# Window attention in a four-layer network: score tiles of 32 rows by 64 columns, value tiles of 32 columns, head parity in place of window as the unit

## The chip, the cores and the metric

The kernel runs on one core of a Trainium2 chip. A core has five engines that work side by side, each through its own list of instructions in order: TensorE (PE; PEld is its weight load), VectorE (DVE), ScalarE (ACT), GpSimd (POOL) and SyncE (SP), which here only loads registers and issues DMA transfers. They meet through semaphores. The metric is the device time of one execution in microseconds, the median of several runs; lower is better.

## What is computed

Four images of 256 channels by 64 by 64 points pass through four layers, each added to its input after a group normalisation: two attention layers and two state-space (Mamba) layers. The change is in the attention layers alone. What matters of their reference:

```python
xw = to_windows(x_img)                    # 8 by 8 windows of 64 points
qkv = xw @ qkv_w.T + qkv_b
q, k, v = (qkv[..., :C], qkv[..., C:2 * C], qkv[..., 2 * C:])
logit = einsum('bpc,bqc->bpq', q.mean(axis=2) * SCALE, k.mean(axis=2))
tk_logit, idx = top_k(logit, 4)           # each window reads 4 windows
k_g, v_g = ...                            # keys and values of these 4
# 8 heads of 32 channels, 64 queries, 4 * 64 keys
attn = softmax(einsum('bphqd,bphkd->bphqk', qh * SCALE, kh), axis=-1)
out = einsum('bphqk,bphkd->bphqd', attn, vh)
out_img = from_windows(out) + lepe(v)     # a 3x3 depthwise convolution of v
out_img = out_img @ wo_w.T + wo_b
```

So a window has 8 heads, and each head a score matrix of 64 queries by 256 keys with a contraction over 32 channels. Everything is float32.

## The kernel before

The images go one after the other (`net_kernel`). Each attention layer has a scan phase (`scan_phase`: recurrence, q, k and v by strips of 8 image columns; keys and values go to a DRAM buffer by window) and then a window phase (`window_phase`), which is where the change lies. There are 4 x 2 = 8 window phases in an execution.

The window phase takes 64 windows as 32 pairs; `i` is the pair, `w` (0 or 1) the window in it, `sj, a = divmod(i, 4)` the strip and the place in it. Channels lie on the 128 partitions in two halves `m`; within a half, `b` is the lower or upper 64 partitions, that is two heads. Per pair the steps are these.

- `indices` (L448) reads the four window numbers of each window into SP's registers; `gather` (L461) issues eight DMAs, four per window, into the tile `kv`, of which there are six. Keys of the four gathered windows lie so that window `j` is on partitions 64*(j mod 2) onward (`r = j % 2`).
- `scores` (L480) makes, for each window, a PSUM tile `sc[w]` of two banks: eight matmuls of 64 rows by 128 columns. The stationary operand is q of two heads side by side (`p h t`), 64 columns each. For this q is held in `qbuf` with a zero in the place of the other head (L105 writes the zeros once per image): a contraction over 64 rows with two heads in it then gives one head's scores in each 64 columns. Two of these matmuls (`r` = 0, 1) sit in different halves of the array's rows and write to different banks.
- `smallest` (L491) takes the minimum over the keys (q is stored negated), `exps` (L502) the exponential in four parts with its sum, into the tile `pr`, of which there are two; `normalise` multiplies by the reciprocal (L512 on DVE, L514 on POOL).
- `turn` (L528) transposes the weights in eight 128 by 128 blocks into two PSUM tiles `pt`; `turned` copies one on DVE (L539) and one on ACT (L541).
- `values` (L552) multiplies by the gathered values, 128 rows by 64 columns, 128 columns of weights moving: two heads' value columns against two heads' weights, so that half of what it makes (a head's values under the other head's weights) isn't used. `own_rows` (L565) therefore picks the used half in four DVE instructions of 32 partitions each and adds it to the image tile `vimg`. There is one PSUM tile `ov`.
- In 26 of the 32 pairs a matmul over a strip follows (`conv`, L208): either `project` of a finished strip, whose result DVE adds to x (L577, `add`), or `queries` for a coming strip, whose result four ACT instructions of 32 partitions write into q (L266, `evict`); SP then copies each half of q to the other partitions (L275, `double`). There are 12 pairs of the latter kind.

The work of a pair overlaps the next: in iteration `i` the loop issues the scores, minima, exponentials and normalisation of pair i + 1 and the turn, values and addition of pair i. The order on each engine is that of the loop, written by hand (L620 to L660): gather(i+2), double, indices(i+3), scores(i+1), smallest(i+1, 0), turn(i, 0), smallest(i+1, 1), exps(i+1, 0) first half, turned(i, 0), exps(i+1, 0) second half, own_rows(i-1), conv, normalise(i+1, 0), turn(i, 1), exps(i+1, 1) first half, turned(i, 1), exps(i+1, 1) second half, add, normalise(i+1, 1), evict, values(i, 0), values(i, 1), and then one or two of the 36 taps of the depthwise convolution that POOL does (L229, L230, L242). Steps of a group normalisation (`gn`, or `stats` in the second layer) are put between them in some pairs (`mids`, `ends`).

PSUM has eight banks: four for `sc`, two for `pt`, one for `ov`, one for `conv` and the normalisation.

Of the kernel before, what the change touches and what calls it, by code (L numbers as in the profile page):

```python
# [18 lines left out]
P = 128  # L19
NB = 4  # L20
C = 256
# [3 lines left out]
NH = 4  # L25
# [20 lines left out]
class Net:  # L46
# [33 lines left out]
    def attention_layers(self, x, w_drams, v_drams):  # L80
        tc, nc = self.tc, self.nc
        with ExitStack() as ctx:
# [17 lines left out]
                [big.tile([P, 2, NW, 2, 64], F32, name=f"q{i}{m}") for m in range(2)]  # L100
                for i in range(2)
            ]
            for t in qbuf[0] + qbuf[1]:
                for r in range(0, P, 32):
                    nc.gpsimd.memset(t[r : r + 32, :, :, 1 - r // 32 % 2, :], 0.0)  # L105
# [151 lines left out]
            def queries(lay, s, m, psum):  # L257
# [4 lines left out]
                def evict():  # L262
                    for h in range(NH):
                        rows = slice(h * 32, h * 32 + 32)
                        b, h2 = divmod(h, 2)
                        nc.scalar.activation(  # L266
                            q[rows, b, :, h2, :].rearrange("p w (j i) -> p w j i", i=8),
                            ps[rows].rearrange("p (j w i) -> p w j i", j=8, i=8),
                            AF.Identity, bias=lay["neg_bq"][rows, m : m + 1], scale=-SCALE,
                        )  # L270
# [163 lines left out]
            def window_phase(lay, work, psum, idx, nxt):  # L434
# [31 lines left out]
                sc = {}  # L466
# [3 lines left out]
                def scores(i):  # L470
                    sj, a = divmod(i, 4)
                    for w in range(2 if i < n_pair else 0):
                        sc[w] = psum.tile([P, 2, 4, P], F32, tag="sc", name="sc", bufs=2)
                        t = kv[i, w]
                        for cq in range(4):
                            m, b = divmod(cq, 2)
                            for r in range(2):
                                rows = slice(r * 64, r * 64 + 64)
                                k0 = b * P + m * 64
                                nc.tensor.matmul(  # L480
                                    sc[w][:, r, cq, :],
                                    qbuf[sj % 2][m][rows, b, 2 * a + w].rearrange("p h t -> p (h t)"),
                                    t[rows, :, k0 : k0 + 64], start=True, stop=True,
                                )

                mn = {}

                def smallest(i, w):
                    if i < n_pair:
                        mn[w] = self.small.tile([P, 4], F32, tag="mn", name="mn", bufs=4)  # L490
                        nc.vector.tensor_reduce(  # L491
                            mn[w], sc[w].rearrange("p r c n -> p c r n"), AX.XY, ALU.min
                        )

                def exps(i, w, part=range(4)):
                    if i < n_pair:
                        if 0 in part:
                            sm[i, w] = self.small.tile([P, 4], F32, tag="sm", name="sm", bufs=4)
                            pr[i, w] = work.tile([P, 4, 2, 2, 64], F32, tag="pr", name="pr", bufs=2)
                        t = pr[i, w]  # L500
                        for cq in part:
                            nc.scalar.activation(  # L502
                                t[:, cq].rearrange("p j r t -> p r j t"),
                                sc[w][:, :, cq, :].rearrange("p r (j t) -> p r j t", j=2),
                                AF.Exp, bias=mn[w][:, cq : cq + 1], scale=-1.0,
                                accum_out=sm[i, w][:, cq : cq + 1],
                            )

                def normalise(i, w):
                    if i < n_pair:  # L510
                        t, s = pr[i, w], sm.pop((i, w))
                        nc.vector.reciprocal(s, s)  # L512
                        t = t.rearrange("p c j r t -> p c (j r t)")
# [7 lines left out]
                def turn(i, w):  # L521
                    pt[w] = [
                        psum.tile([P, 4, P], F32, tag="pt", name="pt_ps", bufs=2) for j in range(2)
                    ]
                    t = pr.pop((i, w))
                    for j in range(2):
                        for cq in range(4):
# [1502 lines left out]
```

## Time and profile before

| | |
|---|---|
| median of 3 runs | 12441.65 us (12438.44 to 12444.25) |
| the profiled execution, its own time | 12439.35 us |
| span of its instructions | 12437.6 us, so 1.75 us lie around it |
| busy share of the span | PE 82%, DVE 82%, POOL 73%, ACT 58% |
| granted TensorE clock, mean | 0.922 |
| first to last scores of a window phase | 228.0 to 496.1 us in the first, 709.7 to 989.8 in the second |
| the same in the other six | 269.7, 281.5, 269.5, 278.3, 269.3 and 278.1 us long |

The eight window phases together are thus some 2200 of 12437.6 us; most of the rest belongs to the two state-space layers. In the page's slices a window phase is where ACT and POOL rise together (slices 2 and 3 of each quarter). The page names groups by line, so L480, L491, L502, L512, L514, L528, L539, L541, L552 and L565 are the attention loop. A line's mean is the time of one instruction as the profiler records it; matmuls overlap, so for PE the distance between starts is what counts, not the mean.

### The profile page before, as it was taken

Reading aid. Unit: us, or ns where it says so; the run is one execution under the profiler, and the core shown is the slowest. Engines: PE = TensorE matmul, PEld = TensorE weight load, DVE = VectorE, ACT = ScalarE, POOL = GpSimd, SP = SyncE. Lnnn points to the kernel's source line nnn. Section 1 sums busy time; section 2 is a strip of 40 time slices with the busy share of each in tenths; the row PEclk is TensorE's granted clock in tenths of the full one; section 3 lists DMA queues with packets and bytes.
Section 4 is the critical chain, followed back from the end, with each engine's and each line's share of the span. In section 5 each row is a group of like instructions: output and inputs, shape, how many; then the busy total and the mean of one; then the engine's idle time right before and its main releaser. Section 6 shows DMA issues by size and latency. Waiting matters only on the chain. (4 is left out here: it accounts for less than half of the span.)

```text
span 12437.6 us, 159552 instructions
## 1 busy us (share of the span) xinstructions
PE 10255.9 (82%) x54592; PEld 6015.9 (48%) x54592; DVE 10216.3 (82%) x9130; ACT 7245.9 (58%) x13300; POOL 9018.9 (73%) x4634
## 2 busy tenths in 40 slices
PE   8987887787898788777789878877878987887777
PEld 4664544443466454444346645444434664544443
DVE  6777898897677799889767779988976777998897
ACT  4565554776466555477645655547754565554775
POOL 4666886887466688688746668868874666886887
PEclk9999998999899999899889999989988999998998
DMA  3343554454334455454433434545543343554454
GB/s 96 108 128 131 168 169 147 167 169 142 97 108 127 132 169 170 146 168 167 144 95 109 127 130 172 169 146 167 169 142 95 109 127 130 172 170 146 167 170 140
DMA packets 680299, 1773.54 MB, mean 143 GB/s; under 512 B 89120, under 2 KB 195120, under 8 KB 678464
## 3 DMA queue, kind: packets, MB, share of 16 engines
q1 hardware_dynamic: 679488, 1763.34, 43.7%
q8 instruction: 435, 7.13, 0.2%
q14 instruction: 376, 3.08, 0.1%
HBM read 1601.51 MB, written 94.37 MB: 136 GB/s over the span
## 5 line engine op out<-in xcount | busy, mean ns | idle before, releaser
L926 POOL TENSOR_TENSOR hc<-h,cb 128x1024 f32<-128x1024 f32 x2056 | 4814.1, 2350 | 988.2 <-DVE h L920 425.6
L920 DVE TENSOR_TENSOR_SCAN h<-da,m_state,pb 128x1024 f32<-128x1024 f32 x1248 | 2919.9, 2340 | 161.7 <-DVE pb L914 2.8
L872 PE MATMUL y<-ident,hc 128*128 128x128 f32 x16384 | 2371.0, 293 | 346.7 <-POOL hc L926 259.0
L872 PEld LDWEIGHTS y<-ident,hc 128*128 128x128 f32 x16384 | 2091.8, 152 | 1009.7 <-POOL hc L926 439.0
L914 DVE TENSOR_TENSOR pb<-du,pb 128x1024 f32<-128x1024 f32 x1672 | 2024.8, 1211 | 92.5 <-PE pb L844 89.3
L856 ACT ACTIVATE da<-delta,m_v 128x1024 f32<-128x1024 f32 x1672 | 1898.8, 1141 | 220.8 <-DVE h L920 204.0
L844 PE MATMUL pb<-m_parts,pick 128*128 128x512 bf16 x3312 | 1099.8, 417 | 872.2 <-DVE h L920 821.8
L502 ACT ACTIVATE pr<-sc,mn 128x256 f32<-128x256 f32 x2048 | 956.6, 478 | 770.8 <-PE pt_ps L528 551.2
L514 POOL TENSOR_TENSOR pr<-pr,sm 128x1024 f32<-128x1024 f32 x512 | 967.9, 1897 | 560.0 <-DVE sm L512 380.6
L844 PEld LDWEIGHTS <-pick 128*128 128x128 bf16 x3312 | 255.2, 101 | 1883.1 <-DVE h L920 1160.3
L920 DVE TENSOR_TENSOR_SCAN h<-da,pb 128x1024 f32<-128x1024 f32 x424 | 969.6, 2287 | 55.6 <-DVE pb L914 1.4
L830 POOL TENSOR_TENSOR bb<-du,bb 128x1024 f32<-128x1024 f32 x376 | 888.8, 2364 | 65.2 <-DMA bb<-m_cd 60.5
L491 DVE TENSOR_REDUCE mn<-sc 128x4 f32<-128x1024 f32 x512 | 609.6, 1219 | 244.9 <-PE sc L480 242.8
L920 DVE TENSOR_TENSOR_SCAN h<-dap,m_state,bb 128x1024 f32<-128x1024 f32 x288 | 672.0, 2333 | 76.2 <-ACT dap L856 63.4
L528 PE MATMUL pt_ps<-ident,pr 128*128 128x128 f32 x4096 | 571.6, 283 | 145.7 <-ACT pts L541 64.3
L208 PE MATMUL conv_ps<-att_y,att_wb 128*128 128x512 f32 x1536 | 688.8, 593 | 0.0
L856 ACT ACTIVATE dap<-delta,m_v 128x1024 f32<-128x1024 f32 x376 | 419.6, 1116 | 422.3 <-DVE h L920 298.2
L552 PE MATMUL ov_ps<-pts,kv 128*64 128x128 f32 x8192 | 583.6, 289 | 91.6 <-DVE vimg L565 75.6
L480 PE MATMUL sc<-kv,q 64*128 64x128 f32 x8192 | 573.0, 288 | 81.7 <-DMA kv<-kv_dram 68.0
L528 PEld LDWEIGHTS pt_ps<-ident,pr 128*128 128x128 f32 x4096 | 465.8, 144 | 315.4 <-issue 151.4
L480 PEld LDWEIGHTS sc<-kv,q 64*128 64x128 f32 x8192 | 515.8, 196 | 124.3 <-issue 56.1
L552 PEld LDWEIGHTS ov_ps<-pts,kv 128*64 128x64 f32 x8192 | 456.4, 141 | 217.2 <-DVE vimg L565 131.9
(270 smaller groups left out, 18063.0 us busy)
## 6 DMA issues: line engine op xcount, KB each, us to landing
cb<-m_cd SPq DMA_DIRECT2D x2048, 512.0 KB
kv<-kv_dram SPq DMA_DIRECT2D x2048, 128.0 KB
bb<-m_cd SPq DMA_DIRECT2D x376, 512.0 KB
q<-q SPq DMA_DIRECT2D x256, 256.0 KB
kv_dram<-kst SPq DMA_DIRECT2D x128, 256.0 KB
kv_dram<-vn SPq DMA_DIRECT2D x128, 256.0 KB
x<-in_x_dram SPq DMA_DIRECT2D x8, 2048.0 KB
m_pe<-in_pe_dram SPq DMA_DIRECT2D x32, 512.0 KB
```

The source lines that it names most:

```text
L480: nc.tensor.matmul(sc[w][:, r, cq, :], qbuf[sj % 2][m][rows, b, 2 * a + w].rearrange("p h t -> p (h t)"), t[rows, :, k0 : k0 + 64], start= ...
L502: nc.scalar.activation(t[:, cq].rearrange("p j r t -> p r j t"), sc[w][:, :, cq, :].rearrange("p r (j t) -> p r j t", j=2), AF.Exp, bias=m ...
L514: nc.gpsimd.tensor_tensor(t, t, s.rearrange("p (a o) -> p a o", o=1).to_broadcast([P, 4, 256]), ALU.mult,)
L528: nc.tensor.transpose(pt[w][j][:, cq, :], t[:, cq, j].rearrange("p r t -> p (r t)"), self.ident,)
L552: nc.tensor.matmul(ov[i][b * 64 : b * 64 + 64, m, :, :, w, :], t[:, j, c0 : c0 + 64], pts[w][j][:, cq, :], start=(j == 0), stop=(j == 1),)
L830: nc.gpsimd.tensor_tensor(pb[i], slots[i][0]["du"], pb[i], ALU.mult)
L844: nc.tensor.matmul(pb[i][:, ss], self.pick[:, n : n + 1].to_broadcast([P, P]), blk["parts"][:, ss], start=True, stop=True,)
L856: nc.scalar.activation(da[i], blk["delta"], AF.Exp, scale=blk["a"](n))
L872: nc.tensor.matmul(blk["y"][:, ss], t[:, ss], self.ident, is_transpose=True, start=(n == 0 and ss.start % NT == 0), stop=(n == DS - 1 and ...
L914: nc.vector.tensor_tensor(pb[i], blk["du"], pb[i], ALU.mult)
L920: nc.vector.tensor_tensor_scan(h[i][:, ss], da[i][:, ss], pb[i][:, ss], state, ALU.mult, ALU.add)
L926: nc.gpsimd.tensor_tensor(hc[i][:, ss], h[i][:, ss], cb[i][:, ss], ALU.mult)
```

## The change

- q is held without zeros: `qbuf` has 64 columns per window instead of 128, the 16 memsets of L105 go, `evict` is two ACT instructions of 64 partitions instead of four of 32, and `double` moves half the bytes.
- The unit of `sc`, `mn`, `pr`, `sm`, `pt` and `pts` is no longer the window `w` but the head's parity `h`: each of the two now holds both windows of the pair. Its four parts are (w, m) instead of (m, b), and the two halves of its partitions are `b` instead of the two heads.
- `scores` makes 32 matmuls of 32 rows by 64 columns instead of 16 of 64 by 128; four row places (r, h) go to four different banks, two column places (b) to the two halves of the partitions. The two `sc` tiles are filled interleaved, all within one block.
- `values` is called once for a pair: 32 matmuls of 128 rows by 32 columns, 64 moving columns, instead of 16 of 128 by 64 with 128. All four heads of a half lie on their own 32 partitions of `ov`, which is half as large.
- `own_rows` is one DVE instruction of 128 partitions instead of four of 32.
- `pr` has four buffers instead of two.
- Sizes of the minima, exponentials, normalisation, transposes and copies stay as they are.

```diff
-                [big.tile([P, 2, NW, 2, 64], F32, name=f"q{i}{m}") for m in range(2)]
+                [big.tile([P, 2, NW, 64], F32, name=f"q{i}{m}") for m in range(2)]
                 for i in range(2)
             ]
-            for t in qbuf[0] + qbuf[1]:
-                for r in range(0, P, 32):
-                    nc.gpsimd.memset(t[r : r + 32, :, :, 1 - r // 32 % 2, :], 0.0)
...
-                    for h in range(NH):
-                        rows = slice(h * 32, h * 32 + 32)
-                        b, h2 = divmod(h, 2)
+                    for b in range(2):
+                        rows = slice(b * 64, b * 64 + 64)
                         nc.scalar.activation(
-                            q[rows, b, :, h2, :].rearrange("p w (j i) -> p w j i", i=8),
+                            q[rows, b].rearrange("p w (j i) -> p w j i", i=8),
...
                 def scores(i):
                     sj, a = divmod(i, 4)
-                    for w in range(2 if i < n_pair else 0):
-                        sc[w] = psum.tile([P, 2, 4, P], F32, tag="sc", name="sc", bufs=2)
-                        t = kv[i, w]
-                        for cq in range(4):
-                            m, b = divmod(cq, 2)
-                            for r in range(2):
-                                rows = slice(r * 64, r * 64 + 64)
-                                k0 = b * P + m * 64
-                                nc.tensor.matmul(
-                                    sc[w][:, r, cq, :],
-                                    qbuf[sj % 2][m][rows, b, 2 * a + w].rearrange("p h t -> p (h t)"),
-                                    t[rows, :, k0 : k0 + 64], start=True, stop=True,
-                                )
+                    if i < n_pair:
+                        for h in range(2):
+                            sc[h] = psum.tile([P, 2, 2, 2, P], F32, tag="sc", name="sc", bufs=2)
+                        for w in range(2):
+                            for m in range(2):
+                                for r in range(2):
+                                    for h in range(2):
+                                        r0 = r * 64 + h * 32
+                                        rows = slice(r0, r0 + 32)
+                                        for b in range(2):
+                                            k0 = b * P + m * 64
+                                            nc.tensor.matmul(
+                                                sc[h][b * 64 : b * 64 + 64, r, w, m, :],
+                                                qbuf[sj % 2][m][rows, b, 2 * a + w],
+                                                kv[i, w][rows, :, k0 : k0 + 64],
+                                                start=True, stop=True,
+                                            )
...
-                            pr[i, w] = work.tile([P, 4, 2, 2, 64], F32, tag="pr", name="pr", bufs=2)
+                            pr[i, h] = work.tile([P, 4, 2, 2, 64], F32, tag="pr", name="pr", bufs=4)
...
-                def values(i, w):
-                    if w == 0:
-                        ov[i] = psum.tile([P, 2, 2, 8, 2, 8], F32, tag="ov", name="ov_ps", bufs=1)
-                    t = kv.pop((i, w))
-                    for m in range(2):
-                        for j in range(2):
-                            for b in range(2):
-                                cq = 2 * m + b
-                                c0 = C + cq * 64
-                                nc.tensor.matmul(
-                                    ov[i][b * 64 : b * 64 + 64, m, :, :, w, :],
-                                    t[:, j, c0 : c0 + 64], pts[w][j][:, cq, :],
-                                    start=(j == 0), stop=(j == 1),
-                                )
+                def values(i):
+                    ov[i] = psum.tile([P, 2, 8, 2, 8], F32, tag="ov", name="ov_ps", bufs=1)
+                    for w in range(2):
+                        t = kv.pop((i, w))
+                        for m in range(2):
+                            for j in range(2):
+                                for h in range(2):
+                                    for b in range(2):
+                                        p0 = b * 64 + h * 32
+                                        c0 = C + m * P + p0
+                                        nc.tensor.matmul(
+                                            ov[i][p0 : p0 + 32, m, :, w, :],
+                                            t[:, j, c0 : c0 + 32],
+                                            pts[h][j][:, 2 * w + m, b * 64 : b * 64 + 64],
+                                            start=(j == 0), stop=(j == 1),
+                                        )
...
-                        for r in range(4):
-                            rows = slice(r * 32, r * 32 + 32)
-                            out = vimg[rows, :, 8 * sj : 8 * sj + 8, 1 + a * 16 : 17 + a * 16]
-                            nc.vector.tensor_tensor(
-                                out, ov[i][rows, :, r % 2].rearrange("p m j w i -> p m j (w i)"),
-                                out, ALU.add,
-                            )
-                        del ov[i]
+                        out = vimg[:, :, 8 * sj : 8 * sj + 8, 1 + a * 16 : 17 + a * 16]
+                        nc.vector.tensor_tensor(
+                            out, ov.pop(i).rearrange("p m j w i -> p m j (w i)"), out, ALU.add
+                        )
...
-                    values(i, 0)
-                    values(i, 1)
+                    values(i)
```

## The prediction

> **What bounds the kernel now.** The chain of waits that ends last covers only 17% of the span and lies in the last image's state-space layers, so it says nothing on the attention loop. I read the page's groups first for sizes, then the timeline of a few pairs for the order, then the waits, then the clock by windows. The page gives the loop's pieces:
>
> ```profile
> L502 ACT ACTIVATE pr<-sc,mn 128x256 f32<-128x256 f32 x2048 | 956.6, 478 | 770.8 <-PE pt_ps L528 551.2
> L514 POOL TENSOR_TENSOR pr<-pr,sm 128x1024 f32<-128x1024 f32 x512 | 967.9, 1897 | 560.0 <-DVE sm L512 380.6
> L552 PE MATMUL ov_ps<-pts,kv 128*64 128x128 f32 x8192 | 583.6, 289 | 91.6 <-DVE vimg L565 75.6
> L480 PE MATMUL sc<-kv,q 64*128 64x128 f32 x8192 | 573.0, 288 | 81.7 <-DMA kv<-kv_dram 68.0
> ```
>
> 8192 records are 32 for each of 256 pairs, where the code has 16 matmuls: each float32 matmul is two passes. ACT's largest wait is for the transposes: with two `pr` buffers an exponential can't be written before `turn` has read the one of a pair earlier. One pair in the timeline (start, length, engine, line):
>
> ```profile
> 407.85 2.06 PE L480 MATMUL sc<-kv,q 64*128 64x128 f32 x32
> 409.05 2.35 DVE L491 TENSOR_REDUCE mn<-sc 128x4 f32<-128x1024 f32 x2 [0.88 <-PE sc L480]
> 409.83 1.09 PE L528 MATMUL pt_ps<-ident,pr 128*128 128x128 f32 x8
> 410.76 1.88 PE L208 MATMUL conv_ps<-att_y,att_wb 128*128 128x512 f32 x4
> 411.01 0.47 ACT L502 ACTIVATE pr<-sc,mn 128x256 f32<-128x256 f32 x1 [0.47 <-PE pt_ps L528]
> 411.33 0.68 DVE L539 COPY pts<-pt_ps 128x512 f32<-128x512 f32 x1
> 411.93 1.71 DVE L565 TENSOR_TENSOR vimg<-ov_ps,vimg 32x256 f32<-32x256 f32 x4
> 412.48 1.04 PE L528 MATMUL pt_ps<-ident,pr 128*128 128x128 f32 x8
> 413.69 2.35 PE L552 MATMUL ov_ps<-pts,kv 128*64 128x128 f32 x32 [0.17 <-DVE vimg L565]
> 415.97 2.06 PE L480 MATMUL sc<-kv,q 64*128 64x128 f32 x32
> ```
>
> From scores to scores it is 8.12 us, and TensorE's starts fill it: scores 1.98, turn 0.93, conv 1.72, turn 1.21 (0.34 of it waiting for `own_rows`), values 2.28 (0.38 waiting for ACT's copy). The loop is bound by TensorE, by little. The third reading is the clock (PE busy, weight loads, DVE, ACT, POOL, then PEclk):
>
> ```profile
> 475.72:479.13 3.41, 1.09 (x8) 0.86 (x8) 2.85 (x4) 0.00 (x0) 3.41 (x3) 1.00 0.51 137
> 479.13:482.55 3.42, 1.76 (x8) 1.57 (x8) 2.66 (x7) 2.42 (x9) 1.17 (x2) 0.50 0.19 66
> ```
>
> A stretch of 3.41 us in which the array had little to do is followed by one at half clock. Over all such stretches of this trace, counting each matmul's streaming time[...] by the share of the rows that it uses, the next one is at half clock below 0.375 of full use (1.28 us of work) and at full clock above, with 11 misses in 3067.
>
> **What the Trainium skill says.** "TensorEngine Tiling (Array Packing)", Tiling Modes: 32 by 64 is a mode of eight tiles, tiles run weight loads and matmuls in parallel, changing the mode drains the array. The trace has two tiles at most: their matmuls start 6 to 7 ns apart in pairs every 112 ns (scores) or 109 ns (values), the second passing the first one's waiting second pass; changes of mode show as steps of 0.2 us. Eight or four at once no run shows. "TensorE: Matmul & The Clock Gate", Part 3, reports 10.6 times for 16 tiles of 32 by 32; its Part 2 gives a floor of about 25 ns between starts, which I keep as a rival. Its Part 1 describes the gate as an idle window of about 3.4 us that halves the clock; the trace agrees, and adds the 0.375.
>
> **The change part by part.**
>
> *Scores.* 64 passes in place of 32. A pass streams 128 columns: 107 ns alone, 112 as paced now. With eight places at once that is eight rounds: 7 x 0.11 + 0.16 (first round, as in values now) = 0.87 us to the last start, with 0.2 for the change of mode 1.07 before `turn` may start, against 1.98. Results lie 1.14 us after the start. Now the first minimum starts 1.2 us after the start, because window 0 is done halfway; with both `sc` tiles filled interleaved it waits for all: same time. Dispatch isn't the bound: 28 PE instructions between two waits of its sequencer take as little as 114 ns, 4 each. If eight run at once: -0.9 us on PE. Bounds: 0.8 us (nothing lost at the change) and 3.6 us (pairs only: 16 pairs x 2 passes x 112 ns).
>
> *Values.* 64 passes of 64 columns, four column places: 16 rounds of 55 ns, 0.92 us, against 1.74 of pure work. But all of it now needs both copies of `turn(i, 1)`: today window 0's half (0.93 us) covers them. So -0.8 of work, and a wait of up to 0.7 in the middle becomes bare.
>
> *own_rows.* One instruction of 0.42 for four (1.71): -1.3 us DVE, and the 0.34 before values goes. *evict*: 2 x 0.69 for 4 (2.75): -1.38 us ACT in 12 of 32 pairs, behind the last exponential, so on nothing's path. *Memsets*: 16 per image, 15.7 us of POOL; hidden behind the load of x but for a wait of the first normalisation of 1.3 us over all images: -1.3. *Double*: half the bytes, the same two issues: nothing. *pr with four buffers*: ACT's wait for `turn` goes.
>
> **What is late next.** Three rings then lie close together.
> - ACT: scores start, +1.15 result, +1.3 first minimum and hand-over, then in its order exp, exp, copy, exp, exp, exp, exp, copy, exp, exp; from 411.01 to 415.89 less the 0.3 wait for turn that goes: 4.6; then the next scores, which now need *both* `sc` tiles free. 1.15 + 1.3 + 4.6 + 0.2 = 7.25 us.
> - SP: eight gathers of 0.655 are 5.24, the register loads 1.75: 7.0; with a double (two of 0.63) 8.26. A gather can start only when values(i-1) freed its buffer, and lands 2.0 us after its issue (third gather issued 707.14, scores 709.73): 7.4 us for a ring.
> - POOL: two normalisations of 1.9 and 36 taps of mostly 2.75 over 27 pairs, 7.2; in second layers 2.48 more in one pair of four.
>
> PE needs 1.07 + 0.93 + 1.72 + 0.93 + 1.0 = 5.7 and isn't the bound. I carried the queues forward over all 32 pairs with these durations, the code's order, the buffers and the clock rule. For the kernel before this gives 167 us for the 21 intervals from the sixth on where the trace has 170.6 (first layer), 180.5 against 182 to 184 (second), 25.6 and 46.4 for the first two and the last five against 25 to 27 and 47, so it is trusted to a few us per phase. For the change: plain pairs 7.3 us, with a double 7.6 to 8.3, mean 7.6. Middle: -8.0 us in first layers, -13.1 in second.
>
> What is given back: the first minimum of a phase waits for both windows' gathers (+1.1). In the six pairs without conv the array has 3.4 us of work in over 7 us, in the worst stretch 0.9 to 1.1 against the 1.28 needed, so they run partly at half clock: +0.8 at the start and -1.4 to +0.7 at the end. With conv the worst stretch has turn and values, 0.87 + 0.85 = 1.72: safe. Ends: -0.5. Per phase -5.7 in the first and -13.3 in the second layer, times four: -76, and -1.3 for the memsets: -77 us. Without the clock rule it would be -115.
>
> 12439.35 - 77 = 12362 for the profiled execution, which lies 2 us under the median: **12365 us**.
>
> **The rivals.**
> - *Too few places at once (slower).* Place: TensorE in scores. If the waiting second passes let only pairs run, scores take 3.6 and values 1.8: PE needs 9.2 us a pair, and the emptier array halves its clock as well: +620 us without the clock, about +1390 with it, 13060 to 13830. If four run at once, scores take 1.8: +119, 12560. With the 25 ns floor (64 x 25 = 1.6 and the change of mode) +121 without and +341 with the clock. It decides from scores of about 1.25 us on, that is with fewer than some seven places (64 x 112 / 7 = 1.0, and 0.2). For it: no trace shows more than two, and the second pass must be overtaken seven times. Against: the second tile's first pass starts 7 ns after the first's, so overtaking works, and the sequencer is seen 34 instructions ahead, as many as a round of eight takes.
> - *No change.* The SP ring and the clock take the rest: scores at 1.2 and values at 1.1 give 0, and a plain pair at 7.6 instead of 7.3 takes some 60 (8 phases x 25 pairs x 0.3) from the gain. 12420 to 12460. For it: three rings within 0.4 us.
> - *More gained.* No half clock, and gathers that land sooner: -115 to -145, 12300 to 12325. Against: the six pairs lack the work.
> - *pr matters alone.* If four buffers weren't felt (the old wait stays), the rest would end at +98, 12540: the exponentials would be held by `turn` as before and the array be emptier. Against: both tiles of a pair and two pairs fit in four.
>
> **How the numbers follow.** Forecast, all eight at once with a gain: 0.58, 12290 to 12415. More gained: 0.05. No change: 0.10. Too few places: 0.20, of which 0.10 up to 12600 and 0.10 far above. Clock or chain worse than reckoned: 0.07, up to 12600. The range reaches from 12290 to 12600, which leaves about 0.13 out. A measurement of this kernel tells about 0.2% (25 us) from no change; chances: faster 0.62, same 0.11, slower 0.27.
>
> **What would show it.** Right: 64 score passes in about 1.1 us and values in about 1.0 from one timeline, ACT's wait for pt_ps gone, scores waiting for ACT or for kv's DMA, pairs of 7.3 to 8.2 us in slices 2 and 3 of each quarter, PEclk below 1 at the ends of a phase. Wrong: passes in pairs 100 ns apart, scores over 1.3 us, or half clock in pairs that have a conv.

## The result and the profile after

The changed kernel takes 12326.35 us (median of 4 runs, 12311.57 to 12329.85), the kernel before 12442.95 us beside it. The ratio is 0.9906 with a 95% interval of 0.9891 to 0.9921: 0.9% faster, beyond the 0.2% that a measurement of this kernel can tell from no change. The profiled execution took 12326.55 us with a span of 12324.8 us, 112.8 us less than before.

These are four groups of the attention loop on the changed kernel's page (line, engine, operation, tiles, shapes, count, then busy time and mean ns of one, then the idle time before them and what ended most of it):

```profile
L501 ACT ACTIVATE pr<-sc,mn 128x256 f32<-128x256 f32 x2048 | 958.0, 490 | 773.0 <-DVE mn L490 555.3
L490 DVE TENSOR_REDUCE mn<-sc 128x4 f32<-128x1024 f32 x512 | 609.7, 1219 | 386.0 <-PE sc L480 386.0
L480 PE MATMUL sc<-kv,q 32*64 32x128 f32 x16384 | 410.5, 300 | 151.5 <-DMA kv<-kv_dram 94.9
L555 PE MATMUL ov_ps<-pts,kv 128*32 128x64 f32 x16384 | 432.4, 234 | 112.4 <-DVE pts L540 65.4
```

ScalarE's largest wait has changed its name: before it waited 551.2 us for the transposes (`pt_ps`), now 555.3 us for the minimum. The sum is nearly the same, so here the size of the wait says nothing; its name says that another ring is closed (a ring is a circle of steps in which each waits for the one before, so that its length is the time of a pair). TensorE has twice the matmuls and is busy with scores for 410.5 us instead of 573.0.

One pair in the timeline of the changed kernel (start, length, engine, line, tiles; in brackets the idle time before it):

```profile
406.86 1.26 PE L480 MATMUL sc<-kv,q 32*64 32x128 f32 x64
...
408.05 1.09 PE L529 MATMUL pt_ps<-ident,pr 128*128 128x128 f32 x8
408.14 2.35 DVE L490 TENSOR_REDUCE mn<-sc 128x4 f32<-128x1024 f32 x2 [1.05 <-PE sc L480]
...
409.46 0.47 ACT L501 ACTIVATE pr<-sc,mn 128x256 f32<-128x256 f32 x1 [1.40 <-DVE mn L490]
...
411.01 0.41 DVE L566 TENSOR_TENSOR vimg<-ov_ps,vimg 128x256 f32<-128x256 f32 x1
...
411.11 1.18 PE L529 MATMUL pt_ps<-ident,pr 128*128 128x128 f32 x8 [0.25 <-ACT pts L542]
...
412.65 0.63 ACT L542 ACTIVATE pts<-pt_ps 128x512 f32<-128x512 f32 x1
...
413.33 0.98 PE L555 MATMUL ov_ps<-pts,kv 128*32 128x64 f32 x52 [0.18 <-ACT pts L542]
...
414.02 1.41 ACT L261 ACTIVATE q<-conv_ps,neg_bq 64x512 f32<-64x512 f32 x2
414.24 1.74 PE L480 MATMUL sc<-kv,q 32*64 32x128 f32 x64
```

From scores to scores it is 7.38 us instead of 8.12. The ring is 1.28 us from the scores' start to the minimum, 1.32 to the first exponential, then ScalarE without a gap from 409.46 until the last exponential ends just before the eviction at 414.02, and the next scores start 0.2 us later. TensorE now has gaps in this pair: the 0.25 and 0.18 us shown, and 0.31 us between the values' first matmuls, which the lines left out hold.

Where the 112.8 us went, by the starts of the scores in both traces (sums over the four images, us):

| piece | before | after | difference | forecast |
|---|---|---|---|---|
| first to last scores, first layers | 1076.6 | 1053.8 | -22.8 | -21 |
| first to last scores, second layers | 1118.0 | 1052.7 | -65.3 | -51 |
| last scores of a first layer to first of the second | 854.9 | 851.5 | -3.4 | -2 |
| last scores of a second layer to the load of the state-space layer's weights | 92.4 | 77.2 | -15.2 | -2 |
| everything else | 9295.6 | 9289.6 | -6.0 | -1 |

The last row isn't touched by the change but for the memsets; in the runs below it lies between 9273 and 9291 us without a known reason, so its 6 us stay unexplained. Below, an interval is the time from one pair's scores to the next, numbered by the pair it starts with; in interval k the loop's iteration k - 1 does its turn, conv and values. The first pair is 0. A plain interval is one that only the ring holds; "the middle" means the 21 intervals from 5 to 25.

### The profile page after: what moved, and what is told of

Read it like the earlier page. It is cut to its first block, busy times and chain, and to the rows that moved or that the text cites. A ratio compares the mean times of both kernels' runs of the same rounds, so it can differ in the third digit from the quotient of the medians.

```text
span 12324.8 us, 191425 instructions
## 1 busy us (share of the span) xinstructions
PE 9979.3 (81%) x70976; PEld 5673.2 (46%) x70976; DVE 9877.7 (80%) x8362; ACT 7059.2 (57%) x13044; POOL 8959.7 (73%) x4570
## 4 chain that ended last, share of the span: by engine, by line
DVE 33%; PE 33%; ACT 16%; issue 9%; POOL 6%; DMA 2%; SPq 2%; DVEq 0%; POOLq 0%; ACTq 0%
DVE h L918 16%; PE conv_ps L204 7%; DVE pb L912 7%; PE y L870 5%; PE u_ps L1205 3%; ACT pr L501 3%; ACT da L854 2%; PE pb L842 2%; DVE lp L240 2%; PE sc L480 2%; DVE mn L490 2%; PE u_ps L1572 2%; SPq L456 1%; POOL pr L515 1%; DMA kv<-kv_dram 1%
## 5 line engine op out<-in xcount | busy, mean ns | idle before, releaser
L501 ACT ACTIVATE pr<-sc,mn 128x256 f32<-128x256 f32 x2048 | 958.0, 490 | 773.0 <-DVE mn L490 555.3
L480 PE MATMUL sc<-kv,q 32*64 32x128 f32 x16384 | 410.5, 300 | 151.5 <-DMA kv<-kv_dram 94.9
L555 PE MATMUL ov_ps<-pts,kv 128*32 128x64 f32 x16384 | 432.4, 234 | 112.4 <-DVE pts L540 65.4
L240 DVE SCALAR_TENSOR_TENSOR lp<-vimg,att_v,lp 128x512 f32<-128x512 f32 x616 | 465.5, 756 | 27.9 <-DVE lp L240 0.5
L859 ACT ACTIVATE m_state<-h 128x1 f32<-128x1 f32 x1536 | 290.6, 192 | 344.2 <-DVE h L918 343.5
## 6 DMA issues: line engine op xcount, KB each, us to landing
kv_dram<-kst SPq DMA_DIRECT2D x128, 256.0 KB
kv_dram<-vn SPq DMA_DIRECT2D x128, 256.0 KB
```

Source lines behind the costliest of these rows:

```text
L501: nc.scalar.activation(t[:, g].rearrange("p j r t -> p r j t"), sc[h][:, :, g // 2, g % 2, :].rearrange("p r (j t) -> p r j t", j=2), AF.E ...
```

## The experiments

My theory after the result: the loop was taken from TensorE to a ring of scores, minimum and ScalarE, with SyncE's gathers close behind. The rivals are these: the gain is that of the side edits (`pr`, `own_rows`) and not of the tiles; TensorE is still the bound; half clock eats a part; in second layers something else holds. In all runs the ratio is to the kernel before, run beside them; its 95% interval is in brackets.

**The side edits undone, one by one and together.**

```diff
-pr[i, h] = work.tile(..., tag="pr", name="pr", bufs=4)
+pr[i, h] = work.tile(..., tag="pr", name="pr", bufs=2)
```

> The changed kernel with two pr buffers instead of four. My theory (the loop is now a ring scores - minimum - ScalarE - scores of 7.38 us, with TensorE in second place): the second tile's first exponential, which starts 4.89 us after the scores, must then wait for the end of turn(i, 1) at 5.4 us, so the ring grows by about 0.6 us; part of it lies under SyncE's own lateness: 12430 to 12510 us, near the kernel before, and ScalarE's wait for pt_ps is back in the profile. Rival (the smaller tiles alone make the gain, since turn now comes earlier): 12326 plus at most 25 us. Rival (the buffers were all the gain): 12500 or more.

Measured: 12430.07 us, ratio 0.9993 [0.9986, 1.0]. The gain is gone. A pair of that run's timeline:

```profile
430.10 1.06 PE L529 MATMUL pt_ps<-ident,pr 128*128 128x128 f32 x8 [0.23 <-issue]
...
430.33 0.49 ACT L501 ACTIVATE pr<-sc,mn 128x256 f32<-128x256 f32 x1
...
431.25 0.47 ACT L501 ACTIVATE pr<-sc,mn 128x256 f32<-128x256 f32 x1 [0.34 <-POOL vimg L226]
...
432.17 0.60 ACT L542 ACTIVATE pts<-pt_ps 128x512 f32<-128x512 f32 x1
...
432.81 0.98 PE L555 MATMUL ov_ps<-pts,kv 128*32 128x64 f32 x52 [0.64 <-ACT pts L542]
```

The second tile's first exponential starts at 431.25, 0.1 us after the last transpose of the pair before (430.10 + 1.06). The profile puts the 0.34 us down to a POOL tap, which has nothing to do with it; the tile that comes free at that moment shows the true releaser. ScalarE's copy comes later by that, and the values wait 0.64 us for it instead of 0.18. From scores to scores many intervals now take 7.85 us. Over the whole page ScalarE's exponentials wait 219.9 us for `pt_ps` again. But the longer ring is the smaller part of the cost: of the 117 us between the two profiled executions the middle of the eight phases holds 42 (1376 us for 1334), and the first and last five intervals of each phase, six of which have no conv, hold 67 (840 for 773). There the half clock grows from 363 to 455 us, so the wait for `turn` and the slow clock act together; they weren't parted.

```diff
-out = vimg[:, :, ...]
-nc.vector.tensor_tensor(out, ov.pop(i)..., out, ALU.add)
+for r in range(4):
+    rows = slice(r * 32, r * 32 + 32)
+    out = vimg[rows, :, ...]
+    nc.vector.tensor_tensor(out, ov[i][rows]..., out, ALU.add)
```

> The changed kernel with own_rows in four instructions of 32 partitions as before (each about 0.43 us). My theory: VectorE's reciprocal and its copy of turn(i, 1) come 1.3 us later, values and the normalisation with them, so the plain pair grows by 0.5 to 1 us: 12400 to 12450 us. Rival (VectorE has slack in the ring of ScalarE): 12326 plus at most 25 us.

Measured: 12422.09 us, ratio 0.999 [0.9982, 0.9999]. This edit undone takes the gain away as well. The timeline of one pair:

```profile
435.38 1.71 DVE L568 TENSOR_TENSOR vimg<-ov_ps,vimg 32x256 f32<-32x256 f32 x4
...
437.12 0.18 DVE L513 RECIPROCAL sm<-sm 128x4 f32<-128x4 f32 x1
...
437.33 0.69 DVE L540 COPY pts<-pt_ps 128x512 f32<-128x512 f32 x1
...
438.08 1.09 PE L555 MATMUL ov_ps<-pts,kv 128*32 128x64 f32 x60 [0.62 <-DVE pts L540]
```

VectorE works from 435.38 to 438.02 without a gap, and its copy of the second turn, which the values need, is the last in the row; they wait 0.62 us for it. The interval takes 7.86 us (431.23 to 439.09).

> The changed kernel with both helpers undone at once: two pr buffers and own_rows in four instructions; what is left is the smaller tiles, the one evict less and the smaller double. My theory (rings: TensorE was relieved of some 2 us a pair, but the wait for turn and VectorE's four instructions lie one behind the other on the ring): no gain at all, 12430 to 12560 us. Rival (each of the two undone edits alone costs the same ring its slack, so that both together cost no more than one): 12420 to 12440 us. Rival (the smaller tiles bring a gain of their own): below 12400 us.

Measured: 12480.92 us, ratio 1.0035 [1.0023, 1.0048]: slower than the kernel before. So in sum the smaller tiles don't pay without the two helpers. The rival that the two cost one and the same slack falls: together they cost some 155 us, one by one 104 and 96 (differences of the medians); that is less than the 200 of both, so a part is shared.

The sum hides two parts of opposite sign. In the middle the smaller tiles do gain alone: a plain interval takes 7.87 us instead of 8.12, and the middle of all phases 1387 us instead of 1413. The first and last five intervals lose more than that, 841 us for 782. Intervals 2 and 3 of the first phase, whose iterations have no conv (busy time of PE, PEld, DVE, ACT and POOL with counts, the granted clock, the DMA share, GB/s), in the kernel before and then in this run:

```profile
254.01:261.86 7.85, 6.15 (x83) 5.24 (x81) 5.41 (x9) 4.69 (x18) 3.76 (x3) 1.00 0.44 129
261.86:269.70 7.84, 6.15 (x82) 5.24 (x81) 5.59 (x10) 4.73 (x19) 6.56 (x5) 1.00 0.48 137
```

```profile
254.82:264.89 10.07, 7.19 (x147) 5.79 (x145) 5.59 (x10) 4.85 (x18) 4.48 (x4) 0.67 0.38 106
264.89:274.96 10.07, 7.20 (x147) 5.71 (x145) 5.58 (x10) 4.84 (x18) 6.54 (x5) 0.67 0.36 107
```

The old tiles, half of whose work wasn't used, kept the clock at 1.00 here; with the smaller ones it falls to 0.67. In the first and last five intervals of all phases this run has 450 us at half clock, the kernel before 222.

What the two helpers would bring to the kernel before wasn't tried, so the rival that they alone make the gain is not refuted. Without its two waits (0.34 and 0.38 us) TensorE's pair of 8.12 us before would be about 7.4 us (an estimate from the prediction's pair), as long as the new ring. But the helpers hang on the tiles: with the old value tiles `own_rows` must pick the used half, and the two additional `pr` buffers (8 KB per partition) found room only because q without zeros is 16 KB smaller (beside the old q 40.5 KB are left for the window phase's tiles, and 48 would be needed). That room is worth more than the 15.7 us of POOL's memsets per image.

**How much TensorE still matters.**

```diff
-for w in range(2):
-    for m in range(2):
-        for r in range(2):
-            for h in range(2):
+for h in range(2):
+    for w in range(2):
+        for m in range(2):
+            for r in range(2):
```

> The changed kernel with the head parity as the outermost loop of scores: four places at once instead of eight, and the first tile is complete after half of the matmuls. My theory (ScalarE's ring bounds, TensorE has more than 1 us to spare): scores take about 1.9 us to turn instead of 1.19, the first minimum starts 1.1 to 1.2 us after the scores as before, and the time stays within 12300 to 12400 us. Rival (TensorE is the bound, as before the change): 0.7 us more in every pair, 12460 to 12490 us. Rival (only pairs of places overlap): scores take 3.6 us or more, 12800 us and above.

Measured: 12327.82 us, ratio 0.9914 [0.9898, 0.9931], as the changed kernel. The timeline of one pair:

```profile
402.08 1.62 PE L480 MATMUL sc<-kv,q 32*64 32x128 f32 x64
...
403.26 2.35 DVE L490 TENSOR_REDUCE mn<-sc 128x4 f32<-128x1024 f32 x2 [0.94 <-PE sc L480]
...
403.63 1.09 PE L529 MATMUL pt_ps<-ident,pr 128*128 128x128 f32 x8
```

With four places at once the scores take 1.55 us to `turn` instead of 1.19, and the minimum starts 1.18 us after the scores instead of 1.28, since its tile is complete earlier. The expected 1.9 us was too long. So the edit does two things at once: it gives TensorE 0.36 us more and makes the ring 0.1 us shorter. The plain interval follows the ring, with 7.26 us instead of 7.38, and not TensorE, which thus isn't the bound there any more. In the total the shorter ring isn't seen. It also means that eight places instead of four save little on TensorE and nothing in time.

**Gathers and SyncE.**

```diff
-kv[i, w] = t = work.tile([P, 2, 2 * C], F32, tag="kv", name="kv", bufs=6)
+kv[i, w] = t = work.tile([P, 2, 2 * C], F32, tag="kv", name="kv", bufs=8)
```

> The changed kernel with eight kv buffers instead of six, so that a gather needn't wait for the values of the pair just before; double stays. If a good part of the lateness in the middle pairs is this wait and not SyncE's own 7.63 us a pair: middle pairs fall to about 7.65 us, 12275 to 12305 us. If it is SyncE's own work alone: within 12 us of 12326.

Measured: 12281.1 us, ratio 0.9875 [0.9858, 0.9891]. SyncE's own waits before a gather in the changed kernel, and then with eight buffers (us in total, times, longest):

```profile
SPq L456 <- PE ov_ps L555: 291.3, 143, 12.1
```

```profile
SPq L456 <- PE ov_ps L555: 99.7, 71, 5.7
```

What it does to the scores (wait for the gathers, the changed kernel and then eight buffers):

```profile
PE sc L480 <- DMA kv<-kv_dram: 94.9, 76, 7.9
```

```profile
PE sc L480 <- DMA kv<-kv_dram: 62.1, 18, 7.6
```

76 late gathers become 18. In first layers the middle falls from 165.8 to 157.7 us, 7.51 us an interval. That is less than the 7.63 us that I had reckoned for SyncE's own work, so that figure was too large. Second layers gain nothing from first to last scores (1055 us for 1053): their intervals 14 and 26 grow from 9.7 and 9.4 to 11.0 and 11.2 us. Some 14 us of the gain lie in the piece "everything else", which has no explanation.

```diff
 for b in range(2):
     rows = slice(b * 64, b * 64 + 64)
-    nc.scalar.activation(q[rows, b]...)
+    for to in range(2):
+        nc.scalar.activation(q[to * 64 : to * 64 + 64, b]...)
...
 def double():
-    for b in range(2):
-        nc.sync.dma_start(q[there, b], q[here, b])
+    pass
```

> The changed kernel without SyncE's two copies of q (double): evict writes each half of q to both places itself, four ScalarE instructions of 64 partitions instead of two, so 1.4 us more ScalarE behind the last exponential in 12 of 32 pairs. My theory (in pairs that aren't 7.38 us it is SyncE that is late: 4 x 7.0 + 2 x 1.26 us in every four pairs): middle pairs fall from a mean of 7.87 to 7.4 to 7.55 us, 12240 to 12280 us. Rival (the lateness is that of the gathers' landing, not of their issue): within 15 us of 12326. Rival (ScalarE's additional 1.4 us is not hidden): 12380 to 12450 us.

Measured: 12307.73 us, ratio 0.9894 [0.9878, 0.9911]. Neither theory has it whole. The first layers do what mine says (the middle falls from 165.8 to 158.7 us), but the second layers rise from 167.6 to 170.0. So SyncE's lateness can be taken away from either side, by its work or by its wait, and a second limit lies in the second layers.

**The second layers.**

```diff
-taps = [t for s in (NW - 2, NW - 1) for t in lepe(lay, s, pool=True)]
+t6, t7 = (lepe(lay, s, pool=True) for s in (NW - 2, NW - 1))
+taps = t6[9:] + t7[9:] + t7[:9]
+mine = dict(zip((2, 3, 4, 7, 8, 11, 12, 15, 16), lepe(lay, NW - 2)))
...
+if i in mine:
+    mine[i]()
-for t in taps[4 * i // 3 : 4 * (i + 1) // 3]:
+for t in taps[i : i + 1]:
```

> The kernel without double (four evictions on ScalarE) and, in addition, nine of POOL's 36 taps given to VectorE (0.94 us each there) in the pairs that have no add; POOL then has 27, one per pair. My theory (without double a first-layer phase is ScalarE's ring at 7.4 to 7.6 us, and a second-layer phase, 264 to 270 us there, is held by POOL: 4 x 7.2 + 2.48 us in every four pairs): second layers fall to 256 to 261 us from first to last scores, first layers stay at 257; 12255 to 12285 us. Rival (second layers are held by the wait of the statistics' own chain over four engines in pairs 14, 18, 22 and 26, not by POOL's load): second layers stay at 264 to 270 us, 12295 to 12315 us.

The edit shown comes on top of the one before (`double` gone).

Measured: 12271.0 us, ratio 0.9869 [0.9853, 0.9886], 37 us less than without the shared taps. Second layers take 258.6 to 263.0 us, first layers, which were to stay at 257, 251.5 to 256.0: POOL's load was part of it, in both, but intervals 18 and 22 of the second layers still take 9.4 and 9.6 us on average. Interval 18 of the first image in this run's timeline:

```profile
842.32 1.26 PE L479 MATMUL sc<-kv,q 32*64 32x128 f32 x64
...
843.60 1.23 DVE L489 TENSOR_REDUCE mn<-sc 128x4 f32<-128x1024 f32 x1 [0.31 <-PE sc L479]
844.92 1.06 ACT L161 ACTIVATE att_xn<-att_xn 128x1024 f32<-128x1024 f32 x1
...
846.01 1.22 DVE L165 TENSOR_REDUCE gn_s<-att_xn 128x4 f32<-128x1024 f32 x1 [1.18 <-ACT att_xn L161]
...
847.15 1.21 DVE L489 TENSOR_REDUCE mn<-sc 128x4 f32<-128x1024 f32 x1
```

Between the two minima stands a step of the statistics (`reduce`, L165). It waits 1.18 us for ScalarE's `square`, which is late because the four evictions come before it, and the second minimum starts 2.3 us later than it could. That is the rival's chain, and the eviction that replaced `double` feeds it.

**The clock.**

```diff
+if i in (0, 1, 2, 27, 28, 31):
+    conv(psum, wb, WQ - 4 * C, y[:, :, strip[0], :]..., 0)
```

> The changed kernel with an additional convolution of the first strip, whose result nobody reads, in the six pairs of a phase that have no conv (0, 1, 2, 27, 28, 31), in the conv's place. My theory (a stretch of 3.41 us with less than 0.375 of array work is followed by one at half clock, and these pairs lose by it): the half clock inside the phases, some 50 us of each, falls by a third or more, above all in the pairs from 26 on, and the time falls by 10 to 40 us, to 12285 to 12315 us, although work was added. Rival (these pairs wait for VectorE, ScalarE and the transfers, and the clock costs nothing): 12326 within 10 us, or 5 to 15 us more for the six times 1.7 us of TensorE.

Measured: 12308.52 us, ratio 0.9896 [0.9879, 0.9912]. The interval overlaps that of the changed kernel, so the time alone doesn't show the gain; the windows do. Intervals 2 and 3 of the first phase again, with the same columns as above, in the changed kernel and then with the additional convolution:

```profile
253.90:262.00 8.10, 5.52 (x148) 4.50 (x144) 4.25 (x7) 4.73 (x18) 4.73 (x4) 0.90 0.48 134
262.00:271.00 9.00, 6.78 (x149) 5.59 (x146) 4.26 (x7) 4.84 (x18) 6.30 (x5) 0.71 0.42 119
```

```profile
253.20:260.60 7.40, 6.55 (x154) 4.51 (x150) 4.08 (x6) 4.73 (x18) 4.54 (x3) 1.00 0.49 144
260.60:268.00 7.40, 6.55 (x155) 4.53 (x152) 4.25 (x7) 4.72 (x18) 6.52 (x4) 1.00 0.51 147
```

Without it the granted clock falls to 0.90 and 0.71, with it it stays at 1.00, and the two intervals take 14.80 instead of 17.10 us. The whole execution spends 1929 us at half clock instead of 2072. Behind the last scores of a second layer it costs 0.9 us (20.2 for 19.3), where the convolution of iteration 31 is in the way.

**Together.**

> Everything that relieved a ring, together: no double, nine taps on VectorE, scores with the head parity outermost, and the additional convolution in the six pairs without one. If each takes its own wait away: 12200 to 12260 us, below the changed kernel and the one before. Rival (one ring is left that all of them share, ScalarE's): no more than the best of the parts, 12260 to 12300 us.

Measured: 12248.15 us, ratio 0.9852 [0.9835, 0.9868]; first layers 247 to 250 us, second 254 to 261. That is 78 us below the changed kernel. One by one `double` gone gave 19, the taps 37, the convolution 18 (not clear of noise) and the order of the scores nothing, some 73 together. So the parts about add up, and no one ring that all share eats them.

```diff
-plan(stats(s, lambda: psum), (ends, 4 * s + 6), (ends, i), (mids, i + 1),
-     (ends, i + 2), (mids, i + 3), (ends, i + 3), (mids, i + 4))
+d = 1 if s < 3 else 0
+plan(stats(s, lambda: psum), (ends, 4 * s + 6), (ends, i), (mids, i + 1),
+     (ends, i + 2 + d), (ends if d else mids, i + 3 + d),
+     (ends, i + 3 + 2 * d), (mids, i + 4 + 2 * d))
```

> The kernel with everything together and, in addition, the statistics of the first three strips of a second layer later: square one pair later, where ScalarE has no eviction, reduce at the end of that pair instead of between the two minima, and the column sums one pair later. If the pairs of 9.6 us of the second layers come from reduce, which waits for ScalarE's square behind the eviction and holds the second minimum: 1.9 us less in each of 3 x 4 pairs, 12215 to 12235 us. If they come from POOL's load: 12248 within 10 us.

Measured: 12276.25 us, ratio 0.9867 [0.985, 0.9883]. The two ratios' intervals overlap, but the pieces are clear: first layers stay (996 us for 994 in sum), second layers go from 1031 to 1069. Intervals 14 and 18 fall from 9.6 to 7.4 us as expected, but 16, 20 and 24 go to over 11. The timeline there:

```profile
827.70 2.78 ACT L262 ACTIVATE q<-conv_ps,neg_bq 64x512 f32<-64x512 f32 x4
...
830.54 0.59 PE L136 MATMUL gn_pv<-gn_s,one_gn 128*128 128x8 f32 x2 [2.55 <-ACT q L262]
```

The column sums need the one PSUM bank that they share with conv. In the iteration where I put them, conv's result is emptied by ScalarE's evictions, so TensorE stands still for 2.55 us with the next scores behind it. I had moved the step past one queue and forgot the bank.

> The same with eight kv buffers. If gathers no longer hold anything once double is gone: within 8 us of the same without. If the last excess over 7.3 us in plain pairs is a gather's wait for a buffer: 15 to 40 us less.

Measured: 12233.3 us, ratio 0.9833 [0.9816, 0.9849]. The buffers bring 43 us here too, with `double` gone: first layers take 241 to 246 us, plain intervals 7.27 to 7.38. Here second layers gain as well (1069 to 1045 us in sum).

```diff
 own_rows(i - 1)
+for t in outs.get(i, ()):
+    t()
...
-     (ends, i + 2), (mids, i + 3), (ends, i + 3), (mids, i + 4))
+     (ends, i + 2), (outs, i + 3), (ends, i + 3), (mids, i + 4))
```

> The kernel with everything together (statistics at their old places) with eight kv buffers, and with reduce issued after own_rows instead of between the two minima. If reduce in its old place holds the second minimum and with it ScalarE (9.6 us pairs 14, 18, 22 and 26 of a second layer): these pairs fall to 7.7 to 8.5 us, second layers from 258 to 247 to 252 us, first layers to 242 to 245 us by the buffers, 12180 to 12215 us. If the delay only moves to VectorE's copy and the values: second layers stay at 255 us or more, 12220 to 12245 us.

The list `outs` holds the step `reduce` in its new place.

Measured: 12185.29 us (5 runs, 12181.99 to 12192.59), ratio 0.98 [0.9787, 0.9814]: 2.0% faster than before, and 132 (by the ratios) to 141 us (by the medians) below the changed kernel. First layers take 243.1 to 243.5 us, second 249.0 to 250.1. Interval 14 of the first image's second layer, which does what interval 18 did above:

```profile
800.05 1.62 PE L479 MATMUL sc<-kv,q 32*64 32x128 f32 x64
...
801.22 2.36 DVE L489 TENSOR_REDUCE mn<-sc 128x4 f32<-128x1024 f32 x2 [0.21 <-PE sc L479]
...
802.65 1.06 ACT L161 ACTIVATE att_xn<-att_xn 128x1024 f32<-128x1024 f32 x1
...
804.42 1.21 DVE L165 TENSOR_REDUCE gn_s<-att_xn 128x4 f32<-128x1024 f32 x1
```

The two minima follow each other, and `reduce` finds its data. The interval takes 8.8 us, more than the 7.7 to 8.5 expected; what is left over 7.4 is ScalarE's `square` (1.06 us) behind the evictions, before the first exponential. There is no run with eight buffers and `reduce` at its old place, so how the 63 us since "everything together" divide between the two edits isn't shown; in the second layers intervals 14, 18, 22 and 26 fell from 9.6 to 8.8 us on average.

## Why the prediction was right, and where its sum was off

Forecast 12365 us, measured 12326: direction and range held, and so did the mechanism (TensorE relieved, ScalarE's ring next, SyncE close behind). The gain came out half as large again (113 instead of 77 us). By its own steps:

- *Scores, eight places at once, 1.07 us to turn instead of 1.98.* Right: 1.19. The sum written down was off by 0.06, since 7 x 0.11 + 0.16 is 0.93 and with the change of mode 1.13. The minimum starts 1.28 us after the scores in the pair shown, 0.1 later than before, where "same time" was forecast.
- *Values 0.92 us of work, but bare to ScalarE's copy.* Right for the work: the last 52 of the 64 passes start within 0.76 us, four every 56 ns. The waits were larger than the 0.7 allowed. The 0.31 and 0.18 us of idle time don't measure them, since matmuls overlap: from the first start to the last it is 1.87 us, 0.95 over the work.
- *own_rows: 1.3 us VectorE, and the 0.34 us before the values go.* Right for the duration (0.41 for 1.71), too small in what hangs on it: undone it costs 96 us (12422 against 12326), since it also holds VectorE's last copy. Of the 88 us between the two profiled executions 46 lie in the middle and 22 behind the last scores of the second layers. The forecast spoke of the old wait alone.
- *pr: ScalarE's wait for turn goes.* Right, and needed: undone it costs 104 us. The rival's price (12540 without it) was too high by 110.
- *Three rings; plain pairs 7.3, mean 7.6.* The plain pair is right (7.38, ScalarE's ring), the mean isn't: 7.9 in the 21 intervals of first layers, so that the middle gained 4.8 us instead of 8.0. The term that was mis-sized is SyncE's. I had priced its work (7.0 and 8.26 us) and the gather's wait for a buffer (7.4) each alone, as if the larger counted; they lie one behind the other, since after a `double` the gather starts late and its landing is late too. With two more buffers the middle takes 157.7 us, 8.1 less, near the forecast's mean (21 x 7.6 is 160). That the first layers' sum in the table came out nearly as forecast is therefore luck: the first five intervals, forecast 1.9 us longer, stayed the same, which made up for more than half of it.
- *Second layers -13.1 in the middle, last five pairs -1.4 to +0.7.* Too small: -15.0 and -3.3. Before, intervals 14, 18, 22 and 26, which hold the statistics, took 11.1 to 11.8 us; they take 8.1 to 9.7 now. They gained 1.4 to 3.7 us each on average, a plain interval 0.74. Which part of it is the shorter chain of the statistics and which the clock wasn't measured apart.
- *Ends -0.5 per phase.* This is the other mis-sized term: the ends behind the second layers gained 3.2 us in three images and 5.6 in the first, 15 in all. Here no other pair hides anything: the last turns, the values, `own_rows` and two convs of the last strip follow one after the other. The timeline of the first image before:

```profile
1005.10 1.72 DVE L565 TENSOR_TENSOR vimg<-ov_ps,vimg 32x256 f32<-32x256 f32 x4
...
1006.88 2.52 PE L208 MATMUL conv_ps<-vimg,att_wb 128*128 128x512 f32 x4 [2.01 <-DVE vimg L565]
...
1010.78 3.78 PE L208 MATMUL conv_ps<-vimg,att_wb 128*128 128x512 f32 x4 [1.39 <-DVE x L577]
```

and after:

```profile
981.67 0.41 DVE L566 TENSOR_TENSOR vimg<-ov_ps,vimg 128x256 f32<-128x256 f32 x1
...
982.14 1.99 PE L204 MATMUL conv_ps<-vimg,att_wb 128*128 128x512 f32 x4 [0.59 <-DVE vimg L566]
...
985.54 1.99 PE L204 MATMUL conv_ps<-vimg,att_wb 128*128 128x512 f32 x4 [1.42 <-DVE x L576]
```

In all four images the last `own_rows` starts 1.94 us sooner after the last scores (13.37 for 15.31), since two more `own_rows` of the pairs before stand ahead of it on VectorE, each 1.3 us shorter now, and it is 1.3 us shorter itself: 3.2 us, on a bare path. The clock counts in the first image alone: there the second conv ran at half clock before, 3.78 us for 1.99, and in the other three both convs were at full clock before as well. That the shorter emptiness is what keeps the clock there is argued from the threshold, not tried.
- *Half clock in the six pairs without conv.* Right: the last five intervals of a phase spend 7 to 17 us at half clock, 0 to 7 before; the first five of all phases together spend 257 us for 199. The result is near the -115 that the forecast gave "without the clock rule", but not for that reason; the rule held, and other terms were larger.
- *Too few places at once (the slower rival).* It put four places at +119 us. With four the time was that of eight: the rival's price took the scores at 1.8 us, where they need 1.55, and left out that in that order the first tile is complete halfway and that the ring bears 0.36 us of TensorE. The side from which the change could have turned slower was another one: the two helpers, without which it ended at 1.0035.
- *More gained.* Its number (12300 to 12325) was the nearest; its reasons, no half clock and gathers landing sooner, didn't come true, so that its number was near is luck.

## What to carry to other kernels

When an engine that bounds a loop is relieved, list every wait that closes a ring around the loop, and undo the helpers one by one: here the smaller tiles gained only with a deeper buffer and a shorter VectorE step, and lost without both. Work taken from the array can also take its clock: look at the granted clock of the stretches where nothing else fills it. Two delays of one queue, its own work and its wait for a buffer, must be added along the chain and not compared. Before moving a step to another place, check which engine empties the bank or buffer that it needs there.

## What the runs showed of the hardware

- Matmuls in different places of the array overlap: in the 88 fastest of the 256 pairs, 64 passes of 128 columns in eight places of 32 rows by 64 columns start within 0.99 us, 16 ns apart on average; in four places they need 1.35 us (the 106 fastest pairs). A conv's passes of 512 columns start 0.43 us apart, so that a pass of 128 columns takes about 107 ns; by this estimate some six of the eight places work at once on average. The floor of about 25 ns between starts that the Trainium skill gives for up to 64 columns ("TensorE: Matmul & The Clock Gate", Part 2, Back-to-back issue gap) doesn't bind from one place to the next: the values' last 52 passes of 64 columns start within 0.76 us, 15 ns apart.
- More array work made a stretch shorter: 14.80 instead of 17.10 us, at a granted clock of 1.00. The threshold of 0.375 that the prediction took from the trace of before holds in the changed kernel too. It is worked out like this: each matmul counts 0.84 ns a column (the 0.43 us for 512 above) times the share of the array that it uses, rows and columns, and the sum is divided by the stretch of 3.41 us. Of some 3000 stretches at full clock in each of three traces (before, changed, additional convolution) fewer than 20 are followed by the other clock than the threshold says.
- A ScalarE instruction may read 64 partitions of PSUM and write the other 64 of q at the same price: 682 ns for the crossed ones with `double` gone, 687 for the straight ones beside them, 689 in the changed kernel.
